# Moving the softmax inverse and two norms to other slots of a hand-ordered transformer block

## The chip, the cores and the metric

The kernel runs on one core of a Trainium2 chip. The core has a matmul engine (TensorE, PE in the profile), three engines for element-wise work (VectorE = DVE, ScalarE = ACT, GpSimd = POOL), and a queue engine (SyncE = SP) that here only issues transfers. ACT and POOL issue transfers too, each in its own instruction order. The metric is device microseconds (us) for one execution. Before the change the median of three runs is 2609.76 us (2608.44 to 2613.68).

## The reference

The input x is 4 sequences of 1024 tokens with 512 features, in float32. The kernel computes one transformer block conditioned on a vector, and adds its input once more at the end:

```
h  = g1(t) * x / sqrt(mean(x*x) + eps) + b1(t)
x1 = x + softmax(q k^T / sqrt(32)) v @ Wo.T      # 16 heads of 32, q, k, v from h
f  = g2(t) * x1 / sqrt(mean(x1*x1) + eps) + b2(t)
y  = x1 + (silu(f @ gate.T) * (f @ hid.T)) @ out.T   # hidden size 2048
return x + y
```

The two divisions of interest are the softmax's (by the sum over the 1024 keys, for each query and head) and the norms' (by a root mean square, for each token).

## The kernel before, in words

Tokens are cut into 8 blocks of 512 (two for each sequence). Everything is held with features on the 128 partitions. Attention goes by **groups** j = 0 to 63: a group is one block, 4 heads (128 feature rows) and 256 queries, so a block has 8 groups. A group has 4 **slots** (UN = 4), one for each 256 keys; the loop `while g < END` runs over slots g = 0 to 267. In the text, the *kind* of a slot is g % 4, and `p` followed by a number is its place in a block of 32 slots (p5 is g = 5 modulo 32; a block's attention starts at g = 32 n). The engines PE, DVE, ACT and POOL run in exactly the order in which the loop's body emits their instructions. SP's order is chosen by a scheduler, by the time at which it thinks each transfer can start.

A slot r passes through the engines as a software pipeline:

- In slot r, `scores` (line 284) multiplies keys by queries on PE, and `keep` (line 291) copies the result from PSUM to one of nine `raw` tiles on ACT. `running_max` (lines 296, 299) follows on DVE.
- In kind 0 of the next group, `max_T` (line 305) transposes the maxima on PE into the same PSUM tile that the scores use, and `parts` (lines 311 to 316) reduces them on DVE. In kind 1, `parts_T` (321) and `spread` (331, copied by ACT at line 332) bring them back as a `shift` to be added.
- Five slots after its scores, `shifted` (337, DVE) adds the shift and `exponential` (340, ACT) takes the exponential. Six slots after, `weighted` (350, PE) multiplies by the values, and `accumulate` (364) lets a transfer issued by POOL add this 1 MB tile into the group's first tile. Three such transfers belong to a group, each waiting for the landing of the one before.
- Three groups later (index j_n in the loop), `sums` (382, PE) sums over keys, after `fold_sum` (372, DVE) has added the halves at the end of the kind 3 before.

The inverse of the sums goes through memory, so that a reciprocal works on 128x8 numbers and not on 128x256: `sums_out` (387) copies and stores 4 KB (line 146, issued by ACT), `take` (152, ACT) loads them compactly, `invert` (157, DVE) takes the reciprocal, `put` (162, ACT) stores, `sums_in` spreads by four transfers of 32 KB (168, SP), and `normalize` (407, DVE) multiplies. Before the change the steps of group j sit in kinds 0, 1, 2, 3 of one group's slots and kinds 0 and 2 of the next: one slot for each transfer. The last two groups take the reciprocal directly on DVE (`inverse`, line 397).

Around the attention two other streams fill PE. Until slot 60 (FS), the projections of keys, queries and values are popped from a queue by `chain`; each batch half is first normalized (first norm: `norm_squares`, `norm_root`, reciprocal at line 613, `norm_scale` at 179, `norm_mod` at 182). From slot 60 on, the feed-forward network runs on the block before, one step for 128 hidden features every two slots (`pair_15` to `pair_4`, which multiply gate and hidden matrices by blocks with sums of blocks, and `contract`; `gate`, `hidden`, `sub_5`, `add_15` are theirs on DVE). Each block also has `project_out` (four chains from slot `go`), its residual, a second norm that goes through memory like the sums (`norm_compact`, `take`, `invert`, `put`, `norm_spread`), and `token_sums` (470 to 476). `pin`, `between` and `after` place a step at the head, middle or end of a slot. After slot 267 only the feed-forward network of the last block is left.

Every matmul of these is recorded at line 106 when it goes through the helper `mm`.

## Time and profile before

| what | value |
|---|---|
| median of 3 runs | 2609.76 us |
| the profiled execution | 2620.56 us, of it 2618.8 us from first to last instruction |
| mean granted clock of PE | 0.976 |
| busy: PE, DVE, ACT, POOL | 2435.8, 1846.6, 1406.9, 172.4 us |
| transfers | 510.64 MB, 195 GB/s |
| steady blocks (slots 96 to 127, for one) | 276.6 us |

PE is busy 93% of the span, so about 183 us of PE idle time and the time at a lowered clock are all that a new order of the same work can take away. The view of waits says which engine waited for whom; the view of windows gives busy time, the granted clock (PEclk) and the transfers' share for any stretch. A slot's length is read from the timeline as the time from the first score matmul (line 284) to the next slot's first.

### The profile page before, as it was taken

Reading aid. Unit: us, or ns where it says so; the run is one execution under the profiler, and the core shown is the slowest. Engines: PE = TensorE matmul, PEld = TensorE weight load, DVE = VectorE, ACT = ScalarE, POOL = GpSimd, SP = SyncE. Lnnn points to the kernel's source line nnn. Section 1 sums busy time; section 2 is a strip of 40 time slices with the busy share of each in tenths; the row PEclk is TensorE's granted clock in tenths of the full one; section 3 lists DMA queues with packets and bytes.
Section 4 is the critical chain, followed back from the end, with each engine's and each line's share of the span. In section 5 each row is a group of like instructions: output and inputs, shape, how many; then the busy total and the mean of one; then the engine's idle time right before and its main releaser. Section 6 shows DMA issues by size and latency. Waiting matters only on the chain. (4 is left out here: it accounts for less than half of the span.)

```text
span 2618.8 us, 71682 instructions
## 1 busy us (share of the span) xinstructions
PE 2435.8 (93%) x31785; PEld 1162.2 (44%) x31785; DVE 1846.6 (71%) x2180; ACT 1406.9 (54%) x1485; POOL 172.4 (7%) x207
## 2 busy tenths in 40 slices
PE   8989999898999999989998999899998999889999
PEld 3333333334544444444444454444444444444444
DVE  2677777766878877887878787887777777843322
ACT  3656676655556655555565565555565556522110
POOL 0000000000000000000000000000000000000000
PEclk9999999999999999999999999999999999999999
DMA  5698898977888888878877888788887888763442
GB/s 193 179 258 231 228 253 236 223 202 188 193 186 205 198 216 197 189 196 221 204 187 191 216 205 190 187 214 209 191 195 189 214 193 198 180 179 103 139 132 90
DMA packets 216386, 510.64 MB, mean 195 GB/s; under 512 B 43407, under 2 KB 84359, under 8 KB 188686
## 3 DMA queue, kind: packets, MB, share of 16 engines
q0 software_dynamic: 28656, 208.68, 41.1%
q1 hardware_dynamic: 166752, 296.56, 35.0%
q8 instruction: 250, 4.10, 0.6%
q10 hardware_dynamic: 20670, 0.83, 0.5%
q14 instruction: 58, 0.48, 0.1%
HBM read 254.82 MB, written 42.48 MB: 114 GB/s over the span
## 5 line engine op out<-in xcount | busy, mean ns | idle before, releaser
L337 DVE TENSOR_TENSOR raw<-raw,shift 128x2048 f32<-128x2048 f32 (+1 forms) x320 | 592.9, 1853 | 158.0 <-ACT shift L332 153.9
L291 ACT COPY raw<-sc 128x2048 f32<-128x2048 f32 x256 | 479.9, 1874 | 200.1 <-PE sc L284 88.4
L340 ACT ACTIVATE raw<-raw 128x2048 f32<-128x2048 f32 x256 | 490.9, 1918 | 110.0 <-DVE raw L337 109.2
L296 DVE TENSOR_TENSOR rmax<-rmax,raw 128x1024 f32<-128x1024 f32 x384 | 469.4, 1222 | 86.6 <-ACT raw L291 81.7
L106 PE MATMUL pc<-h,ow 128*32 128x512 f32 x4096 | 468.8, 595 | 0.0
L106 PE MATMUL pa<-x,fw 128*32 128x256 f32 x6144 | 394.1, 387 | 30.2 <-ACT shift L332 30.0
L284 PE MATMUL sc<-kq 32*128 32x256 f32 x4096 | 298.3, 406 | 2.8 <-ACT raw L291 2.8
L364 POOL DMA_DIRECT2D raw<-raw x192 | 165.3, 861 | 2040.3 <-ACT raw L340 991.7
L350 PE MATMUL av<-raw,v 128*32 128x256 f32 x4096 | 283.2, 394 | 9.2 <-ACT raw L340 9.2
L106 PEld LDWEIGHTS pa<-x,fw 128*32 128x32 f32 x6144 | 201.2, 111 | 182.7 <-ACT shift L332 40.5
L106 PE MATMUL pa<-sums,fw 128*32 128x256 f32 x4096 | 276.7, 388 | 0.0
L284 PEld LDWEIGHTS sc<-kq 32*128 32x128 f32 x4096 | 187.3, 186 | 143.7 <-issue 87.4
L106 PE MATMUL pkq<-y,wkq 128*32 128x512 f32 (+1 forms) x1664 | 238.3, 607 | 10.2 <-DMA wkq<-in_kq_w 6.0
L106 PEld LDWEIGHTS pc<-h,ow 128*32 128x32 f32 x4096 | 129.0, 110 | 243.2 <-issue 218.7
L106 PEld LDWEIGHTS pa<-sums,fw 128*32 128x32 f32 x4096 | 141.2, 113 | 88.3 <-issue 8.8
L350 PEld LDWEIGHTS av<-raw,v 128*32 128x32 f32 x4096 | 120.8, 111 | 121.8 <-issue 39.2
L538 ACT ACTIVATE t<-pa 128x512 f32<-128x512 f32 x128 | 78.0, 609 | 139.8 <-PE pa L106 136.9
L332 ACT COPY shift<-sp 128x512 f32<-128x512 f32 x128 | 75.0, 586 | 145.1 <-PE sp L331 96.6
L521 ACT COPY pb<-pa 128x256 f32<-128x256 f32 x128 | 45.8, 358 | 194.8 <-PE pa L106 178.8
L106 PE MATMUL pb<-sums,fw 128*32 128x256 f32 x2048 | 137.7, 387 | 12.9 <-DVE pb L528 12.9
L311 DVE TENSOR_REDUCE top<-mt 128x8 f32<-128x1024 f32 x64 | 78.3, 1223 | 96.8 <-PE mt L305 96.8
L559 DVE SCALAR_TENSOR_TENSOR res<-pc,res 128x512 f32<-128x512 f32 x128 | 88.3, 690 | 73.3 <-PE pc L106 73.3
(100 smaller groups left out, 1987.9 us busy)
## 6 DMA issues: line engine op xcount, KB each, us to landing
raw<-raw POOLq DMA_DIRECT2D x192, 1024.0 KB, 9.0
fw<-sw SPq DMA_DIRECT2D x256, 256.0 KB
ow<-in_out_w SPq DMA_DIRECT2D x128, 256.0 KB
fw<-in_gh_w SPq DMA_DIRECT2D x128, 256.0 KB
wkq<-in_kq_w SPq DMA_DIRECT2D x32, 512.0 KB
v<-vs SPq DMA_DIRECT2D x32, 512.0 KB
fw<-in_gh_w SPq DMA_DIRECT2D x128, 128.0 KB
kq<-kqs SPq DMA_DIRECT2D x31, 512.0 KB
```

What stands on the lines that cost most here:

```text
L106: nc.tensor.matmul(dst[k : k + n, :], w[:, k : k + n], moving, start=start, stop=stop, skip_group_check=seeded)
L284: nc.tensor.matmul(sc[:, i, k, :], t[rows, kt * P : (kt + 1) * P], t[rows, q0 : q0 + HQ], start=True, stop=True)
L291: nc.scalar.copy(raw[r].rearrange("p k h q -> p h k q"), state.pop(("sc", r)))
L296: nc.vector.tensor_tensor(rmax[j], rmax[j], raw[r][:, k, :, :], ALU.max)
L311: nc.vector.tensor_reduce(top, state.pop(("mt", j)), AX.X, ALU.max)
L332: nc.scalar.copy(shift[j][:, k : k + 2, :], pp)
L337: nc.vector.tensor_tensor(t, t, s.unsqueeze(1).to_broadcast(list(t.shape)), ALU.add)
L340: nc.scalar.activation(raw[r], raw[r], AF.Exp)
L350: nc.tensor.matmul(av[j][i * DH : (i + 1) * DH, :], v[m][:, kt, i * DH : (i + 1) * DH], raw[r][:, k, i, :], start=(kt == 0), stop=(kt == K ...
L364: nc.gpsimd.dma_start(out=acc[j].rearrange("p k h q -> p (k h q)"), in_=raw[r].rearrange("p k h q -> p (k h q)"), accum_op=ALU.add,)
L538: nc.scalar.activation(state["t", p], bank_a[p], AF.Tanh, scale=0.5)
L559: nc.vector.scalar_tensor_tensor(r, pp, 0.5, r, ALU.mult, ALU.add)
```

## The change

Seven things are done.

1. **Sums behind values.** In kind 0, `sums` is issued after `weighted` and `accumulate`, not ahead of them.
2. **Two slots for each transfer.** The inverse of a group's sums now takes: kind 0 `sums_out`; kind 2 `take`; end of kind 3 `invert`; next group's kind 0 `put`; end of its kind 1 `sums_in`; head of its kind 3 `normalize`.
3. **The last group of each block** (j % 8 == 7, and the last two) does not go through memory: DVE takes the reciprocal of the copied 128x256 tile in kind 1, and `normalize` follows in kind 2. `oT` is allocated by whichever of two groups comes first.
4. **Output projection** starts one slot earlier (`go` from g0 + 14 to g0 + 13), and in kind 1 its first chain comes after `pair_3`.
5. **Second norm** starts two slots earlier and is spread out: squares at p15 and p16, root at p17, load at p19, reciprocal at p20, store at p21, spread at p22, scaling by halves at p24 and p25; the first of the token sums at p25.
6. **First norm.** Its steps are aligned so that scaling falls into kind 2 (before: kind 0 for five of six), and it no longer follows the chain's start exactly; the two extra slots ahead of the last twelve chains are gone.
7. **Before slot 60**, the transposed maxima (`max_T`, `parts`) come ahead of the chain's eviction and the norm's steps.

```diff
+    def near(j: int):
+
+        return j % (C * NB // HQ) == C * NB // HQ - 1 or j >= NR // UN - 2
+
     def sums_out(j: int):
         t = sb.tile([P, HQ], F32, tag="rec", name=f"total{j}", bufs=2)
         nc.scalar.copy(t, state.pop(("sum", j)))
-        compact(f"s{j}", t, DH, HQ)
+        if near(j):
+            state["rec", j] = t
+        else:
+            compact(f"s{j}", t, DH, HQ)
...
-        if qh == 0:
+        if (n, hg) not in oT:
...
             s = math.ceil((len(queue) + 1) / PACE)
-            if s > BS + 15:
-                s += 2
+            s4 = s - 4 - (s - 6) % UN
             tag = f"a{b}_{half}"
-            pin(max(s - 10, 0), load_y, b, half)
+            pin(max(s4 - 6, 0), load_y, b, half)
             for k in range(2):
-                after(s - 8 + k, lambda b=b, half=half, tag=tag, k=k: norm_squares(y[b, half], tag, k))
-            between(s - 6, norm_root, tag)
-            after(s - 5, lambda tag=tag: nc.vector.reciprocal(state[tag], state[tag]))
+                after(s4 - 4 + k, lambda b=b, half=half, tag=tag, k=k: norm_squares(y[b, half], tag, k))
+            between(s4 - 2, norm_root, tag)
+            after(s4 - 1, lambda tag=tag: nc.vector.reciprocal(state[tag], state[tag]))
             for c in range(C):
-                between(s - 4, lambda b=b, half=half, tag=tag, c=c: norm_scale(y[b, half], tag, c))
-                after(s - 4 + c // 2, lambda b=b, half=half, c=c: norm_mod(0, b, y[b, half], c))
+                between(s4, lambda b=b, half=half, tag=tag, c=c: norm_scale(y[b, half], tag, c))
+                after(s4 + c // 2, lambda b=b, half=half, c=c: norm_mod(0, b, y[b, half], c))
...
-        go = g0 + (14 if n < NBLK - 1 else 8)
+        go = g0 + (13 if n < NBLK - 1 else 8)
...
-            after(g0 + 18, add_res, n)
+            after(g0 + 16, add_res, n)
             for k in range(2):
-                after(g0 + 17, lambda n=n, tag=tag, k=k: norm_squares(x2[n], tag, k))
-            between(g0 + 19, norm_root, tag)
-            between(g0 + 19, norm_compact, tag)
-            after(g0 + 20, take, tag)
-            between(g0 + 22, invert, tag)
-            after(g0 + 22, put, tag)
-            between(g0 + 24, norm_spread, tag)
+                after(g0 + 15 + k, lambda n=n, tag=tag, k=k: norm_squares(x2[n], tag, k))
+            between(g0 + 17, norm_root, tag)
+            between(g0 + 17, norm_compact, tag)
+            after(g0 + 19, take, tag)
+            between(g0 + 20, invert, tag)
+            after(g0 + 21, put, tag)
+            after(g0 + 22, norm_spread, tag)
             for c in range(C):
-                after(g0 + 25, lambda n=n, tag=tag, c=c: norm_scale(x2[n], tag, c))
-            for c in range(C):
-                between(g0 + 26, lambda n=n, c=c: norm_mod(1, n // QB, x2[n], c))
-            for i in range(3):
+                after(g0 + 24 + c // 2, lambda n=n, tag=tag, c=c: norm_scale(x2[n], tag, c))
+                after(g0 + 24 + c // 2, lambda n=n, c=c: norm_mod(1, n // QB, x2[n], c))
+            after(g0 + 25, token_sums, n, 0)
+            for i in range(1, 3):
                 after(g0 + 26, token_sums, n, i)
...
-            if kind == 0 and n_on:
-                sums(j_n)
-                if j_n >= direct:
-                    inverse(j_n)
+            if kind == 3 and o_on and not near(j_o):
+                normalize(j_o)
+            if kind == 2 and n_on and near(j_n) and j_n < direct:
+                normalize(j_n)
             if x_on and kind != 1:
                 shifted(r_x)
...
-            if kind == 0 and n_on and j_n >= direct:
-                normalize(j_n)
-            if kind == 2 and o_on:
-                normalize(j_o)
-            if kind == 1 and n_on and j_n < direct:
-                take(f"s{j_n}")
             for fn, a in pinned.pop(g, []):
                 fn(*a)
             if v_on:
                 weighted(r_v)
                 accumulate(r_v)
+            if kind == 0 and n_on:
+                sums(j_n)
+                if j_n >= direct:
+                    inverse(j_n)
+                    normalize(j_n)
...
-            if kind == 3 and n_on and j_n < direct:
-                put(f"s{j_n}")
-            if kind == 0 and o_on:
-                sums_in(j_o)
+            if kind == 1 and n_on and near(j_n) and j_n < direct:
+                nc.vector.reciprocal(state["rec", j_n], state["rec", j_n])
+            if kind == 2 and n_on and not near(j_n):
+                take(f"s{j_n}")
+            if kind == 0 and o_on and not near(j_o):
+                put(f"s{j_o}")
...
+                if kind == 0 and m_on:
+                    columns[0] = P
+                    max_T(j_m)
+                    parts(j_m)
                 if evict is not None:
                     evict()
                 for fn, a in halfway.pop(g, []):
                     fn(*a)
-                if kind == 0 and m_on:
-                    columns[0] = P
-                    max_T(j_m)
-                    parts(j_m)
...
-                if due or len(queue) > FG:
-                    chain(g)()
+                extra = due or len(queue) > FG
                 if kind == 3:
+                    if extra:
+                        chain(g)()
                     pair_7(p)
                     sub_5(p)
                 pair_3(p)
+                if kind == 1 and extra:
+                    chain(g)()
...
-            if kind == 2 and n_on and j_n < direct:
+            if kind == 3 and n_on and not near(j_n):
                 invert(f"s{j_n}")
+            if kind == 1 and o_on and not near(j_o):
+                sums_in(j_o)
```

## The prediction

> **What bounds the kernel now.** First the page, for what is busy:
>
> ```profile
> PE 2435.8 (93%) x31785; PEld 1162.2 (44%) x31785; DVE 1846.6 (71%) x2180; ACT 1406.9 (54%) x1485; POOL 172.4 (7%) x207
> ```
>
> PE bounds it. What can be won is its idle time (183 us) and time at a lowered clock: a mean of 0.976 over 2618.8 us is 63 us lost. Second the view of waits, cut to PE: who keeps it waiting?
>
> ```profile
> PE sum L382 <- issue: 36.0, 17, 7.5
> PE pa L106 <- ACT shift L332: 30.0, 11, 3.9
> PE sum L382 <- PE sc L284: 21.7, 23, 1.0
> PE pt L321 <- DVE split L316: 14.1, 6, 3.1
> PE pb L106 <- DVE pb L528: 12.9, 6, 2.2
> PE sum L382 <- DVE raw L372: 9.6, 9, 4.2
> ```
>
> The three `sum` rows make 67.3 us; then eleven stalls behind the shift copy. Third the timeline around one of each. A kind 1 (slot at 937.0):
>
> ```profile
> 942.76 0.32 ACTq L152 DMA_DIRECT2D fews<-sumss  x1
> ...
> 943.13 0.58 ACT L332 COPY shift<-sp 128x512 f32<-128x512 f32 x1 [4.19 <-DMA rec<-invss]
> ...
> 943.76 1.93 PE L106 MATMUL pa<-x,fw 128*32 128x256 f32 x16 [3.13 <-ACT shift L332]
> ```
>
> ACT stands at the issue of `take` (L152) and the copy queued behind it is late; PE waits 3.13 us, and then 16 matmuls take 1.93 us, where 16 of this size take 1.07 in the next fence. The releaser named is not the load's own input but the spread of another group. A kind 0:
>
> ```profile
> 1201.89 1.15 PE L284 MATMUL sc<-kq 32*128 32x256 f32 x16
> ...
> 1202.74 1.22 DVE L372 TENSOR_TENSOR raw<-raw 128x1024 f32<-128x1024 f32 x1
> ...
> 1204.06 0.64 PE L382 MATMUL sum<-raw,ones_sum 128*32 128x256 f32 x8 [1.02 <-PE sc L284]
> ...
> 1204.49 1.07 PE L350 MATMUL av<-raw,v 128*32 128x256 f32 x16
> ...
> 1205.26 1.87 ACT L291 COPY raw<-sc 128x2048 f32<-128x2048 f32 x1 [3.17 <-DMA raw<-raw]
> ```
>
> PE waits for DVE's fold while the values' matmuls, ready, stand behind. And `keep` waits until a 1 MB accumulation has landed. Fourth the windows (us, busy PE, PEld, DVE, ACT, POOL, clock, DMA share, GB/s): a steady block and the stalled kind 1.
>
> ```profile
> 894.50:1171.10 276.60, 259.70 (x3648) 130.46 (x3644) 218.57 (x257) 160.95 (x164) 21.48 (x25) 0.98 0.83 201
> ...
> 937.00:947.70 10.70, 7.57 (x101) 3.65 (x100) 4.99 (x5) 5.52 (x8) 0.86 (x1) 0.84 0.92 236
> ```
>
> DMA is at 0.83 and DVE at 218.57 of 276.6: both near enough to be next. Slot lengths from the timeline, undisturbed: kinds 0 to 3 take 9.91, 6.19, 7.24, 6.39 us.
>
> **The change, part by part.** Sums are against the profiled execution's 2620.56 us (10.8 above the median of 2609.76).
>
> *Two slots for each transfer.* Eleven kind-1 slots (p5, p25) last 46.6 us more than 11 x 6.19: 30.0 idle, the rest at a lowered clock. `take` goes to kind 2, a slot later; the spread goes to the end of kind 1, `put` to kind 0. The stores L146 landed in a median of 6.3 us, `put` in 7.8, each spread in 6.4 (latest 12.5; my reading of the semaphores' updates in the trace); a pair of slots is 13.6 us or more, so these waits go. What is late next: after p5 the accumulation chain. At p4 one took 12.4 us (1205.7 to 1218.1), the next 10.2; p8's `keep` needs the following one, which would share the DMA engines with them once PE comes 4.8 us earlier. I return 2 us for each of five blocks: 46.6 - 10 = 36.6.
>
> The Trainium skill ("DMA: Bandwidth & Descriptors", Anatomy of one DMA) puts a fixed cost of some 2.0 us on a transfer, which speaks against the change: a 4 KB store would be back within one slot, and two slots would win nothing here, so this term would be zero and the forecast 37 us later. [...]
>
> The lowered clock is in rows: PEclk 0.84 over the slot with a 3.13 us wait, and 0.76 over 1137.20 to 1151.30 after a wait of 2.12. The skill ("TensorE: Matmul & The Clock Gate", What's actually happening) lets the clock halve only after an idle window of about 3.4 us; by that most of these stalls would cost their idle time alone, 30.0 and not 46.6, and the term would be 20.
>
> *Sums behind values.* Values take 1.07 us and the fold ends about 0.9 us behind the scores, so up to 1.07 of each wait goes. But the transposed maxima of the same slot need `keep`'s PSUM tile. At 1207.2 they started 0.09 after `keep`'s end: PE would wait there instead. Taken slot by slot, the smaller of the wait and this slack sums to 27.6 us (4.1 before slot 64, 23.6 after; p0 and p4 give nothing, p28 1.07 each). Bounds 0 and 67.3; I take 24, as p8's 3 us fall under the return above.
>
> *Last group by VectorE.* Seven reciprocals of 128x256. Rows: 1758 ns (L397, from PSUM) and half of 3346 (L613, 128x512): 1.67 to 1.76 each, 12.3 in all, less 7 x 0.19. 49 transfers go. It stands in kind 1 behind the shift, with 2.2 us of DVE idle in an undisturbed kind 1 but 0.19 in kind 2, so kind 2's shift and exponential are late by over 1 us; the values in kind 3 have 0.94 of slack. Cost 0 to 12; I take 0.8 each: -5.6.
>
> *Second norm.* Six slots p27 are 19.7 us over 6.39, six p28 18.6 over 9.91 (7.5 of it in sums). There DVE does 2.74 us of scaling at once and three token sums, on top of the stall at p25. A group needs 27.5 us of DVE in 29.7; with scaling and token sums 33. Spread over p24 to p27 that still leaves about 3.5 us late per block: 30.8 - 21 = 10. Bounds 0 and 31. Its root moves from p19 to p17 with its 0.86 us of PE, its add (POOL) two slots up; SP's 256 KB spread moves from p24 to p22, ahead of p24's loads: cost nothing while SP waits for buffers anyway.
>
> *Output projection.* At p17 PE waits 1.57 us for the bank that the shift copy empties; behind `pair_3` the copy is done. 6 x 1.57 = 9.4; bounds 0 and 9.4, I take 8.
>
> *First norm.* Five pairs of slots with scaling in kind 0 last 26.8 us over 10.85 + 6.17, and slots 48 to 53, the one case with scaling in kind 2, 11.8 over undisturbed ones. One with kind 0, where DVE is busy 13.56 of 14.00 us and PE waits for it:
>
> ```profile
> 396.10:410.10 14.00, 10.78 (x95) 4.83 (x91) 13.56 (x18) 7.24 (x8) 1.72 (x2) 1.00 0.96 276
> ```
>
> Now 3.35 us of reciprocal and 2.74 of scaling fall into kinds 1 to 3, where DVE idles about 3 us; kind 0 idles 4.0. Some 3.3 us per norm stay: 38.6 - 20 = 18. Bounds: 38.6 if nothing is late, -32 if all six cost as slots 48 to 53 did (70.8). Loading y two to four slots earlier costs nothing where its buffer is empty; at slot 8 SP may stand a slot for it, with weights queued behind that PE's chains need two slots later. The maxima ahead of the norm's steps are what frees kind 0; behind them only evictions wait. The two dropped slots change nothing: the queue empties at 1.5 chains a slot behind the first projection, and the last twelve chains come out from slot 54 either way.
>
> *New waits.* `normalize` at the head of kind 3 holds back shift and exponential if the spread, issued one slot earlier, lands late; ACT's `take` now holds back `keep`. Rows: DVE waited 2.2 us once for a spread. Bounds 0 and what rival C prices; I take -8.
>
> Sum: 36.6 + 24 - 5.6 + 10 + 8 + 18 - 8 = 83. 2620.6 - 83 = 2537.6 profiled; less 10.8, **2527**.
>
> **Rivals.** *A, DMA sets the pace.* 0.83 share in a steady block would be 0.88 at 262 us; `keep` waited 81.0 us for accumulations already. Half of the first two terms, 10 for second norm and projection together, 5 for the first norm, and 15 for new waits: 23 + 12 - 6 + 10 + 5 - 15 = 29, so 2581. For it: p0 and p4 have no slack today. Against: p12 and p24 have 0.8 to 1.9.
>
> *B, everything fits.* No return at p5, sums 27.6, second norm 25, po 9, first norm 33, no new waits: 139, so 2471. Against it DVE's 27.5 of 29.7.
>
> *C, slower: the wait moves along with `take`.* The stalled ACT was released by a spread's landing, not by its own input. The spread now ends kind 1 and `take` opens kind 2; if ACT must again see a spread landed, it stands there with `keep` behind it and PE's next scores behind that, in up to 55 groups and not in eleven. Without the first term and the 8, the rest wins 54, so 1.0 us per group decides; at half of today's 4.6 it is 55 x 2.3 = 127 - 54: 2683. Against: the spread needed only 6.4 us, and today most `take`s issue without a stall.
>
> *D, no difference*, if gains and new waits cancel.
>
> **How the numbers follow.** Mine 0.60 (2495 to 2560), A 0.17, B 0.09, C 0.11, D 0.03. The range 2480 to 2600 leaves out C and most of B. A measurement tells 0.2% (5 us) from no change: faster 0.86, same 0.03, slower 0.11.
>
> **What would show it.** Waits of PE for `shift` (30.0) near zero; `sum` rows under 20 us, with some 15 more at `mt`; `pt` gone; steady blocks near 264 us; the clock's mean at 0.985 or more. Wrong if ACT waits at L152, or DVE at L407, in most groups, if `keep`'s wait for accumulations doubles, or if the values wait for the exponential in kinds 3 and 0.

## The result: no difference, and the profile after

The changed kernel takes 2616.32 us (median of 20 runs, 2604.63 to 2635.56), the kernel before 2616.57 (20 runs, 2608.44 to 2623.24) on the same chip. The ratio is 1.0002, with a 95% interval of 0.9984 to 1.002. A gain of 83 us was forecast and none came: the forecast of 2527 us is wrong, and the time lies outside its range of 2480 to 2600; rivals A (2581) and C (2683) miss it too, and only D, with 0.03, has the right time.

The profiled execution of the changed kernel took 2608.14 us, of it 2606.3 us of span, at a mean granted clock of 0.981 (before: 2620.56, 2618.8, 0.976). These two executions lie 12 us apart where the medians are equal; stretches of them are compared below with this in mind.

The page of the changed kernel, engines:

```profile
PE 2433.4 (93%) x31749; PEld 1143.4 (44%) x31749; DVE 1855.9 (71%) x2180; ACT 1405.5 (54%) x1483; POOL 172.9 (7%) x207
```

PE is idle for 173 us of the span, after 183. The stalls named by the prediction did go, so others came. The view of waits cut to PE, changed kernel (us in total, times, longest):

```profile
PE mt L305 <- ACT raw L291: 42.8, 28, 3.5
PE sum L382 <- issue: 24.7, 18, 6.4
PE av L350 <- ACT raw L340: 17.3, 21, 1.5
PE pmf L106 <- DVE h L550: 15.1, 6, 2.5
PE sp L331 <- ACT mT L323: 11.8, 8, 1.7
PE sc L284 <- ACT raw L291: 9.5, 6, 2.7
...
PE sum L382 <- DVE raw L372: 3.0, 3, 1.7
```

The 30.0 us at the shift copy and the 14.1 at `pt` are gone, and the rows of `sum` fell from 67.3 us to 27.7. In their place PE waits 42.8 us at the transposed maxima (`mt`) and 9.5 at the scores for the same thing, `keep`. In the kernel before these two rows were:

```profile
PE mt L305 <- ACT raw L291: 5.2, 7, 2.6
...
PE sc L284 <- ACT raw L291: 2.8, 3, 1.5
```

What `keep` itself waits for is in the page's list of groups; this is its row (busy, mean ns, then idle time ahead of it and what ended most of that) in the kernel before, and then in the changed one:

```profile
L291 ACT COPY raw<-sc 128x2048 f32<-128x2048 f32 x256 | 479.9, 1874 | 200.1 <-PE sc L284 88.4
```

```profile
L291 ACT COPY raw<-sc 128x2048 f32<-128x2048 f32 x256 | 479.3, 1872 | 277.3 <-DMA raw<-raw 153.7
```

Of `keep`'s idle time before, the largest share (88.4 of 200.1 us) was ended by PE's scores; 81.0 us ended with a transfer, as the prediction quotes. Now transfers end 153.7 us of it: the landing of 1 MB accumulations. By the times of these landings, 138.4 us (46 waits) are those of kind 0 and 15.4 us (8 waits) those of kind 1; before, all 81.0 us (35 waits) were those of kind 0. In each of them the accumulation is that of the slot seven back.

Windows of the changed kernel (us, busy PE, PEld, DVE, ACT, POOL, clock, DMA share, GB/s): the same steady block as before (slots 96 to 127), and slots p24 and p25 of the next block.

```profile
871.10:1149.30 278.20, 260.05 (x3648) 127.90 (x3644) 219.48 (x257) 160.69 (x164) 21.55 (x25) 0.98 0.82 198
1357.00:1371.70 14.70, 11.87 (x138) 5.50 (x134) 8.71 (x14) 4.58 (x5) 0.86 (x1) 0.88 0.95 253
1371.70:1381.30 9.60, 7.88 (x101) 3.65 (x100) 5.70 (x7) 6.46 (x8) 0.86 (x1) 0.82 0.68 145
```

The block takes 278.2 us where 264 were forecast and 276.6 were measured before. Slot p24, 11.07 us long in the kernel before, is 14.6 here, with the DMA engines at 0.95 and the clock at 0.88. Its timeline, with the slot ahead of it:

```profile
1351.09 0.86 POOL L364 DMA_DIRECT2D raw<-raw  x1 [9.94 <-ACT raw L340]
...
1352.72 0.32 SPq L263 DMA_DIRECT2D kq<-kqs  x1
...
1353.38 0.84 SPq L264 DMA_DIRECT2D kq<-kqs  x1
...
1357.05 1.15 PE L284 MATMUL sc<-kq 32*128 32x256 f32 x16
...
1359.15 0.64 PE L382 MATMUL sum<-raw,ones_sum 128*32 128x256 f32 x8
...
1362.43 1.87 ACT L291 COPY raw<-sc 128x2048 f32<-128x2048 f32 x1 [5.17 <-DMA raw<-raw]
...
1364.35 1.59 PE L305 MATMUL mt<-ident,rmax 128*128 128x128 f32 x8 [2.83 <-ACT raw L291]
```

In kind 3 POOL issues a 1 MB accumulation (1351.09). Slot p24 starts at 1357.05, values and sums are issued without a wait, and then `keep` stands for 5.17 us until that accumulation has landed (1362.33, by the semaphore's updates), because it writes into the tile that the accumulation reads. The maxima behind it need `keep`'s PSUM tile: PE idles 2.83 us. The accumulation took 11.2 us in the company of the keys' and queries' loads (768 KB, L263 and L264) and the second norm's spread, all issued within 4 us.

Where the time went is seen in slots. The table gives the mean length of stretches of a block, over the five blocks from slot 64 to 223 (from the starts of the score matmuls in the timeline), and the start of slot 64; the lower rows belong to the experiments. "Four parts" are parts 1, 2, 6 and 7 of the change.

| kernel | p0-3 | p4-8 | p9-12 | p13-19 | p20-23 | p24-28 | block | slot 64 |
|---|---|---|---|---|---|---|---|---|
| before | 32.2 | 47.9 | 30.8 | 66.2 | 30.3 | 51.0 | 278.2 | 608.5 |
| changed | 31.7 | 47.1 | 31.2 | 69.8 | 30.2 | 49.8 | 279.7 | 584.6 |
| sums alone | 32.1 | 46.2 | 30.1 | 66.2 | 30.1 | 49.2 | 273.6 | 596.6 |
| two slots alone | 33.0 | 45.3 | 30.8 | 66.2 | 31.3 | 47.9 | 274.3 | 603.4 |
| first norm alone | 32.0 | 47.8 | 30.8 | 66.2 | 30.3 | 51.1 | 278.0 | 588.6 |
| four parts | 32.0 | 46.8 | 30.3 | 66.2 | 31.1 | 47.3 | 273.5 | 589.8 |
| + last group | 32.2 | 47.1 | 31.2 | 66.1 | 31.2 | 47.3 | 274.9 | 590.2 |
| + projection | 32.0 | 47.5 | 31.5 | 68.6 | 30.0 | 47.6 | 277.0 | 595.1 |
| four parts, parted tiles | 30.9 | 44.2 | 30.4 | 66.5 | 31.7 | 46.2 | 269.7 | 584.4 |
| changed, parted tiles | 31.1 | 43.3 | 31.4 | 70.5 | 30.1 | 45.6 | 271.8 | 584.5 |
| best | 30.9 | 41.3 | 30.6 | 66.5 | 32.0 | 44.3 | 265.5 | 584.1 |
| four parts, half transfers | 29.9 | 41.2 | 29.9 | 66.2 | 29.7 | 45.6 | 262.4 | 564.0 |

(p29 to p31 take 19.8 or 19.9 in all of them.) Where the text gives the mean of a single slot, it is over six blocks, slots 64 to 255. The changed kernel is 24 us ahead at slot 64 and loses 1.5 us in each of these blocks; its profiled execution is one of its faster ones. The best kernel and the one with parted tiles and the spread norm alone have the same code up to slot 64 and start it at 584.1 and 589.8, so the last column is good to some 6 us.

### The profile page after: what moved, and what is told of

Same layout as the page of the kernel before. It is cut to its first block, busy times and chain, and to the rows that moved or that the text cites. A ratio compares the mean times of both kernels' runs of the same rounds, so it can differ in the third digit from the quotient of the medians.

```text
span 2606.3 us, 71466 instructions
## 1 busy us (share of the span) xinstructions
PE 2433.4 (93%) x31749; PEld 1143.4 (44%) x31749; DVE 1855.9 (71%) x2180; ACT 1405.5 (54%) x1483; POOL 172.9 (7%) x207
## 3 DMA queue, kind: packets, MB, share of 16 engines
q0 software_dynamic: 28656, 208.68, 41.4%
## 5 line engine op out<-in xcount | busy, mean ns | idle before, releaser
L291 ACT COPY raw<-sc 128x2048 f32<-128x2048 f32 x256 | 479.3, 1872 | 277.3 <-DMA raw<-raw 153.7
L106 PE MATMUL pc<-h,ow 128*32 128x512 f32 x4096 | 476.9, 603 | 2.3 <-DVE rec L404 2.1
L106 PE MATMUL pa<-sums,fw 128*32 128x256 f32 x4096 | 269.5, 380 | 0.0
L350 PEld LDWEIGHTS av<-raw,v 128*32 128x32 f32 x4096 | 108.0, 110 | 143.1 <-issue 49.9
L106 PEld LDWEIGHTS pkq<-y,wkq 128*32 128x32 f32 (+1 forms) x1664 | 74.4, 119 | 147.4 <-issue 122.6
```

The lines of the kernel that those rows point to most:

```text
L106: nc.tensor.matmul(dst[k : k + n, :], w[:, k : k + n], moving, start=start, stop=stop, skip_group_check=seeded)
L291: nc.scalar.copy(raw[r].rearrange("p k h q -> p h k q"), state.pop(("sc", r)))
L350: nc.tensor.matmul(av[j][i * DH : (i + 1) * DH, :], v[m][:, kt, i * DH : (i + 1) * DH], raw[r][:, k, i, :], start=(kt == 0), stop=(kt == K ...
```

## The experiments

All medians are of several runs beside the kernel before on the same chip. Gains are given as (1 - ratio) x 2616 us, so that runs of different chips can be compared; the 95% intervals of the ratios are some 0.002 to either side, 4 to 7 us. The kernels with half transfers leave out half of each tile that is added, so their sums over keys are incomplete.

| kernel | us | ratio, 95% interval | gain, us |
|---|---|---|---|
| changed | 2616.32 | 1.0002 (0.9984 to 1.002) | 0 |
| sums alone | 2578.02 | 0.985 (0.9827 to 0.9872) | 39 |
| two slots alone | 2593.27 | 0.9915 (0.9888 to 0.9942) | 22 |
| first norm alone | 2599.24 | 0.9926 (0.9903 to 0.995) | 19 |
| four parts (1, 2, 6, 7) | 2574.89 | 0.9833 (0.9807 to 0.9858) | 44 |
| + last group by VectorE (3) | 2584.80 | 0.9873 (0.9848 to 0.9897) | 33 |
| + projection (4) | 2592.43 | 0.9903 (0.988 to 0.9925) | 25 |
| changed, kind 0's order altered | 2613.58 | 0.9987 (0.9965 to 1.001) | 3 |
| changed, `norm_mod` later | 2598.64 | 0.9941 (0.9923 to 0.9958) | 15 |
| before, half transfers | 2543.36 | 0.9728 (0.9704 to 0.9752) | 71 |
| four parts, half transfers | 2479.96 | 0.9489 (0.9466 to 0.9511) | 134 |
| changed, half transfers | 2512.31 | 0.9594 (0.957 to 0.9618) | 106 |
| four parts, load pinned to p10 | 2571.97 | 0.984 (0.9816 to 0.9864) | 42 |
| before, parted tiles | 2610.55 | 0.9987 (0.997 to 1.0004) | 3 |
| four parts, parted tiles | 2545.95 | 0.9742 (0.9719 to 0.9765) | 67 |
| changed, parted tiles | 2558.02 | 0.9793 (0.9774 to 0.9811) | 54 |
| four parts, parted, load moved | 2536.58 | 0.9702 (0.9687 to 0.9717) | 78 |
| four parts, parted, norm spread | 2534.79 | 0.97 (0.9683 to 0.9716) | 78 |
| best: all three | 2523.12 | 0.9657 (0.9636 to 0.9678) | 90 |

### The parts one at a time

The theory after the first look at the traces was that of an exchange of tiles. The nine `raw` tiles come back in the order in which they are freed. Before, kind 1's `keep` took the tile that the sums had just freed, and had no transfer to wait for; in the changed kernel it takes the tile of the slot seven back, whose accumulation was issued only one slot earlier.

The first edit was meant to bring the old order back:

```diff
             if v_on:
                 weighted(r_v)
-                accumulate(r_v)
             if kind == 0 and n_on:
                 sums(j_n)
...
+            if v_on:
+                accumulate(r_v)
```

> The changed kernel with one order altered: in kind 0 the sums come behind the values but ahead of `accumulate`, as the freed tiles then come back in the order of before: kind 1's `keep` gets the group's first tile and not the one whose 1 MB transfer was issued a slot earlier. Theory T (tiles): the lost gain sits in this exchange. The wait of `keep` for transfers falls from 153.7 us to 100 or less, PE's waits for `keep` ahead of scores (9.5) and for the exponential ahead of values (17.3) mostly go, and the time is 15 to 30 us under the changed kernel's 2616, so 2586 to 2601. Theory P (pace): the transfers of a group are late as a chain, whichever tile is asked for first; the time stays within 0.3% of 2616 and PE's wait at the transposed maxima (42.8) stays or grows.

Measured: 2613.58 us, ratio 0.9987, no difference that counts. But the edit did not do what it was for: in its trace kind 1's `keep` still waits for the accumulation of the slot seven back (at slot 133, 3.18 us until 1209.00, issued 1195.4). So it says nothing for or against the exchange; it only shows that the order of the sums and `accumulate` costs nothing that can be measured.

The other three take one part each into the kernel before. Sums alone:

```diff
-            if kind == 0 and n_on:
-                sums(j_n)
...
                 weighted(r_v)
                 accumulate(r_v)
+            if kind == 0 and n_on:
+                sums(j_n)
```

> The kernel before with part 1 alone: sums behind values and behind `accumulate`. The prediction's term says 24 us faster than before, 2592. Theory T: the exchange of tiles comes with this part, so `keep`'s wait for transfers goes from 81.0 to some 130 us or more and the 67 us of PE's waits at the sums come back at the transposed maxima and at the next scores: 2608 to 2625. Theory P says 2605 to 2616, with the wait moved to the maxima of the same slot but `keep`'s row little changed.

Two slots for each transfer alone (the projection's chains stay at p15 and p17):

```diff
-            if kind == 2 and o_on:
-                normalize(j_o)
-            if kind == 1 and n_on and j_n < direct:
-                take(f"s{j_n}")
...
+            if kind == 3 and o_on:
+                normalize(j_o)
...
+            if kind == 2 and n_on and j_n < direct:
+                take(f"s{j_n}")
+            if kind == 0 and o_on:
+                put(f"s{j_o}")
```

> The kernel before with part 2 alone: two slots for each transfer of the sums' inverse, all groups through memory; the output projection's first chain moves from slot 14 to 15 since the last group is normalized a slot later. The prediction's terms say 36.6 less 8 for new waits, so about 28 us faster: 2588. Theory T: nothing is exchanged here, so the gain is there: 2580 to 2595, with the 30.0 us at the shift copy gone. Theory P: the time stands at 2605 to 2616, since p5 runs into the chain of transfers at p8 and the gain is lost by then.

First norm alone (parts 6 and 7, as in the change's diff):

> The kernel before with parts 6 and 7 alone: the first norm aligned, and the transposed maxima ahead of evictions before slot 60. The prediction's term is 18 us; in the changed kernel's trace slot 64 starts 24 us earlier, of which the sums' part has some 4. So 2592 to 2600 if what is won there stays won: nothing behind slot 64 differs. If it is lost again behind slot 64 (a later start of transfers or of the clock), 2610 to 2616.

Measured: gains of 39, 22 and 19 us. Theory T fell with the first of them: sums alone carry the exchange of tiles too (one `keep` of kind 1 waits there for the accumulation of the slot seven back, 0.7 us; none did before), and win more than the prediction gave them. PE's waits with sums alone:

```profile
PE sum L382 <- issue: 15.0, 7, 6.4
...
PE mt L305 <- ACT raw L291: 11.1, 14, 1.6
...
PE sum L382 <- DVE raw L372: 0.8, 1, 0.8
```

The three `sum` rows went from 67.3 us to 15.8, and only 5.9 of it came back at `mt` (5.2 to 11.1). Each part does, alone, about what was forecast for it or better (24, 28.6 and 18 us); the sum of the three gains is 81 us, uncertain by some 11.

### The parts together

Four kernels lead from the three parts to the whole change: four parts; with the last group by VectorE (`near` as in the change); with the projection one slot earlier; and, as the last, the changed kernel itself, which adds the second norm. Beside them stands the changed kernel with halved accumulations:

```diff
-                out=acc[j].rearrange("p k h q -> p (k h q)"),
-                in_=raw[r].rearrange("p k h q -> p (k h q)"),
+                out=acc[j][:, 0, :, :].rearrange("p h q -> p (h q)"),
+                in_=raw[r][:, 0, :, :].rearrange("p h q -> p (h q)"),
```

> The kernel before with parts 1, 2, 6 and 7, all groups through memory; the output projection stays in slots 15 and 17 and the second norm where it was. Alone these parts won 40.8 (sums), 25.5 (two slots) and 19.5 us (first norm). Theory A (adding): the gains add, 86 us, so 2525 to 2545, and parts 3 to 5 cost some 80 us. Theory C (collision): two freed stalls run into the same chain of transfers, so 2555 to 2580 and parts 3 to 5 cost the other half. Theory N: nothing is left once parts 1 and 2 meet, 2600 or more, and parts 3 to 5 cost little.

> The same with part 3 as well: the last group of a block inverted by VectorE, the output projection's weights asked for at slot 11 as before. The prediction's cost for part 3 is 5.6 us; the changed kernel's slot 10 is 0.8 us longer in each of six blocks, 4.9 in all. Theory A and N: 3 to 8 us over the kernel without part 3. Theory C, if the 49 fewer transfers make room: 0 to 10 us under it.

> The same with part 4 as well, so the changed kernel with only the second norm in its old places. By the prediction part 4 wins 8 us. If parts 3 to 5 cost what the result lacks and the second norm is the costly one (its squares, root, spread and scaling move PE's waits to slot 17 and the transfers to slot 24), this one is 30 us or more under the changed kernel's 2616. If the output projection in slot 13 is the costly one (the changed kernel's slots 13 to 19 take 44.5 us and not 41.8, 16 us in six blocks), this one is within 10 us of 2616.

> The changed kernel with each 1 MB `accumulate` cut to its first half, 0.5 MB: the second halves of three of four tiles are left out of the sums over keys, so this part of the computation is missing. Everything is issued in the same order. If late accumulations are what the changed kernel waits for, `keep`'s wait for transfers falls from 153.7 us to under 40, and the time falls by the 42.8 us at the maxima, most of the 9.5 and 17.3, and some clock: 2540 to 2565. If the order of PE's and VectorE's own work is what costs, 2590 to 2616.

Measured: the four parts together win 44 us, not 81: Theory C, a collision, though at its edge. Parts 3, 4 and 5 then cost 10, 8 and 26 us one after the other (differences of the gains, each uncertain by some 8), and the change is at zero. The second norm is the costliest, but not alone.

The collision is seen in the table. In the five steady blocks sums alone, two slots alone and both together take 273.6, 274.3 and 273.5 us: the second of the two edits wins nothing there. Ahead of slot 64 the gains are 11.9, 5.1 and 19.9 alone and 18.7 together. Together the waits look like this, in the timeline of slots p4 to p6 of one block (four parts):

```profile
1173.91 1.87 ACT L291 COPY raw<-sc 128x2048 f32<-128x2048 f32 x1 [3.39 <-DMA raw<-raw]
1174.04 0.33 SPq L418 DMA_DIRECT2D res<-in_x  x1
1174.33 0.86 POOL L364 DMA_DIRECT2D raw<-raw  x1 [9.11 <-issue]
...
1187.69 1.86 ACT L291 COPY raw<-sc 128x2048 f32<-128x2048 f32 x1 [2.90 <-DMA raw<-raw]
...
1188.20 0.86 POOL L364 DMA_DIRECT2D raw<-raw  x1 [13.01 <-DMA raw<-raw]
...
1189.61 1.15 PE L284 MATMUL sc<-kq 32*128 32x256 f32 x16 [1.85 <-ACT raw L291]
```

At p4 `keep` is late by a first accumulation (3.39). The next is issued at 1174.33, in one breath with the 1 MB load of the residual (L418), and lands at 1187.67, after 13.3 us. Kind 1's `keep` needs its tile and stands 2.90 us; PE's next scores, behind it, 1.85. The kernel before had the same company at p4 (load at 1205.39, accumulation at 1205.68, 12.4 us), and PE did not wait for it there: the stall that `take` caused in p5 was time in which these transfers caught up. Without it, PE meets them one slot later.

With half transfers the changed kernel falls by 106 us to 2512.31, more than was expected of it. The row of accumulations in the page's list of DMA issues (KB each, median us to landing), whole and halved, and `keep`'s row, halved:

```profile
raw<-raw POOLq DMA_DIRECT2D x192, 1024.0 KB, 9.0
```

```profile
L291 ACT COPY raw<-sc 128x2048 f32<-128x2048 f32 x256 | 479.4, 1873 | 162.3 <-PE sc L284 124.4
...
raw<-raw POOLq DMA_DIRECT2D x192, 512.0 KB, 5.6
```

`keep` now mostly waits for PE's scores, 124.4 of its 162.3 us, and for accumulations 5.6 us, after 153.7. They are what the changed kernel waits for. But halving them helps any version, so two more kernels were halved, and the suspected load was pinned to another slot:

> The kernel before with each `accumulate` cut to its first half, as was done to the changed kernel (2616 to 2512): the second halves of three of four tiles are missing from the sums over keys. If the transfers of the accumulations are what swallows the change's gain, the change is worth its 83 us once they are short: 2512 + 83 = 2595, so 2580 to 2605 here. If the change had no gain to swallow, this kernel falls by the same 104 us as the changed one: 2505 to 2525.

> The kernel with parts 1, 2, 6 and 7 (2575) with each `accumulate` cut to its first half: the second halves of three of four tiles are missing from the sums. It tells whether parts 3 to 5 cost by themselves or through late transfers. By themselves: 2512 less the 41 us between 2575 and 2616, about 2471. Through transfers alone: 2505 to 2515. From the changed kernel's rows, what stays without transfers is slot 10 (0.8), the projection and root in slots 13 to 19 (2.7) and the wait at slot 25 (2.7), less what slots 27 and 28 win (3 to 4): 1 to 3 us in each of six blocks, so I expect 2495 to 2510.

Measured: before 2543.36, four parts 2479.96, changed 2512.31. With short transfers the change wins 35 us (gains 71 and 106), the four parts 63, and parts 3 to 5 cost 28 by their own order. That is more than the 1 to 3 us a block I gave them: the blocks differ by 4.6 us (262.4 and 267.0), of it 4.3 in p13 to p19. It is not the 83 either, in part because short transfers already free `take`: in the halved kernel before p5 lasts 6.19 us, and nothing is left there to win.

```diff
-        pin(g0 + 6, load_res, n)
+        pin(g0 + (10 if n < NBLK - 1 else 6), load_res, n)
```

> The kernel with parts 1, 2, 6 and 7 (2575), with one transfer of each of the first seven blocks moved: the 1 MB load of the residual is pinned to slot 10 and not 6. In the trace that load was issued at slot 4 together with an accumulation that then took 13.3 us, where the others take 8 to 9. Theory: this company is what makes the maxima of slot 4, the scores of slot 6 and the maxima of slot 8 late (slots 4 to 8 take 46.7 us in the mean, and 40.6 with halved accumulations). Then slots 4 to 8 lose 3 to 5 us a block and the time is 2545 to 2560. If the accumulations are late there for another reason, or the load disturbs slots 10 to 12 as much, 2570 to 2580.

Measured: 2571.97 us, no gain, and the load did not move. SP still issued it at p4 (1170.76 in this trace), beside an accumulation of 13.4 us. SP's order is the scheduler's; the pin moved the call, not the transfer. What the load's company costs stayed open with this run.

### Parting the tiles

Kind 0's `keep` takes the tile of slot g - 7, whose accumulation POOL issued in the kind 3 just before (so at p24 above, and at slot 132 in the four-part kernel: issued 1164.4, landed 1173.8). This was so before the change too. The edit gives the first tiles of groups, which the sums set free, three buffers of their own, and the others six:

```diff
-        raw[r] = sb.tile([P, 2, HG, HQ], F32, tag="raw", name=f"raw{r}", bufs=RAW)
+        first_of = r % UN == 0
+        raw[r] = sb.tile(
+            [P, 2, HG, HQ], F32, tag="acc" if first_of else "raw", name=f"raw{r}", bufs=3 if first_of else RAW - 3
+        )
```

> The kernel with parts 1, 2, 6 and 7 (2575), with the nine tiles parted: three for the first tiles of groups, six for the others. Kind 0's `keep` then takes the tile that the sums of the same slot set free, and no longer the one whose accumulation was issued a slot earlier; kinds 1 to 3 take tiles whose accumulation was issued two slots earlier. Theory: PE's waits at the maxima (26.6), the scores (9.3) and part of those at the values (28.0), and the clock behind them, are this order of tiles; `keep`'s wait for transfers falls from 119 us to under 40 and the time to 2530 to 2555. Against it: `keep` of kind 0 then stands behind PE's sums, which end some 3 us into the slot, so the maxima may be as late as today in every group: 2575 to 2600.

> The changed kernel, all seven parts, with the tiles parted: three for the first tiles of groups, six for the others. The kernel with parts 1, 2, 6 and 7 fell by 29 us to 2546 by this edit. If parts 3 to 5 cost only through late accumulations, which this takes away, 2540 to 2555. If they cost by their own order too, as with halved accumulations (2512 against 2480, 32 us), 2570 to 2585. If the changed kernel's loss is all in that order, 2605 or more. Slot 24, 14.0 us in the changed kernel, should be under 11, and slot 25 stay at 8.9 or more.

> The kernel before with only the tiles parted: three for the first tiles of groups, six for the others. By my present theory the order of tiles became the bound when the other stalls went: before, `keep` waited 81 us for transfers, but PE only 5.2 us at the maxima and 2.8 at the scores, so 2600 to 2616 here, and the stalls at `take` and the sums stay. Rival: it held the kernel before as much as the changed one, hidden in the waits named `sum`: 2560 to 2590.

Measured: four parts 2545.95 (a gain of 67 and no longer 44), changed 2558.02 (54 and no longer 0), before 2610.55 (3, within its interval of no change). So the order of tiles did not hold the kernel before, it took 23 us of the four parts' gain and 54 of the changed kernel's. What parts 3 to 5 cost beside it is 13 us, between the two cases that were expected. In the trace of the changed kernel with parted tiles, slot p24 reads:

```profile
1333.24 0.86 POOL L367 DMA_DIRECT2D raw<-raw  x1 [9.99 <-ACT raw L343]
...
1334.05 0.32 SPq L263 DMA_DIRECT2D kq<-kqs  x1
...
1338.32 1.15 PE L284 MATMUL sc<-kq 32*128 32x256 f32 x16
...
1340.72 0.38 PE L385 MATMUL sum<-raw,ones_sum 128*32 128x256 f32 x1
...
1341.14 1.87 ACT L294 COPY raw<-sc 128x2048 f32<-128x2048 f32 x1 [2.62 <-PE sum L385]
...
1343.06 1.09 PE L308 MATMUL mt<-ident,rmax 128*128 128x128 f32 x8 [0.23 <-ACT raw L294]
```

The accumulation issued at 1333.24 landed only at 1346.1, later than in the fence of the changed kernel (12.9 us), and nobody waits for it here: `keep` starts with the end of the sums (2.62 us of idle time on ACT, for PE), and PE waits 0.23 us at the maxima. Cut to PE, the waits are (lines moved by three, so L308 is `mt` and L294 is `keep`):

```profile
PE sum L385 <- issue: 28.6, 23, 6.4
PE pmf L106 <- DVE h L553: 15.1, 6, 2.5
...
PE av L353 <- ACT raw L343: 12.6, 14, 1.5
PE mt L308 <- ACT raw L294: 11.8, 46, 0.3
...
PE sc L284 <- ACT raw L294: 1.0, 1, 1.0
```

`mt` falls from 42.8 to 11.8, and the scores from 9.5 to 1.0. The price is 0.23 to 0.3 us in nearly every group at the maxima (46 times). The edit also takes kind 1 from the tile of seven slots back to that of eight; by the waits above (138.4 and 15.4 us) nearly all of it should be kind 0's, but no run parted the two.

### The residual's load and the second norm

Issued by ACT, whose order is the program's, the load does move (in blocks 1 to 6):

```diff
+        if 0 < n < NBLK - 1:
+            after(g0 + 9, load_res, n)
+        else:
+            pin(g0 + 6, load_res, n)
...
+        queue = nc.scalar if 0 < n < NBLK - 1 else nc.sync
+        queue.dma_start(out=res[n], in_=x[n])
```

> Parts 1, 2, 6 and 7 with parted tiles (2546), and the 1 MB load of the residual issued by ACT at the end of slot 9 in blocks 1 to 6, so that it does move. Theory: its company makes slots 4 and 7 to 8 late (11.86, 7.18 and 11.55 us, against 10 to 10.6, 6.39 and 10.1 with halved accumulations). Then 3 to 4 us a block go: 2524 to 2532. If the load makes slots 10 to 12 late instead, 2540 to 2550.

Measured: 2536.58 us; 11 us more than with parted tiles alone (gains 78 and 67, the intervals of the ratios do not meet). Slots p4 to p8 fall from 44.2 to 41.4 us, the 41.2 of half transfers, and the accumulation at p4 takes 9.4 us in the block shown above (slot 132) and not 13.2. p9 to p12 rise by 0.5. The gain is a little less than expected. The load was not moved in the kernel before, so how much of these 11 us that one would win too is not known.

Two runs look at the second norm. In the changed kernel, its last ACT step issued later:

```diff
-                after(g0 + 24 + c // 2, lambda n=n, c=c: norm_mod(1, n // QB, x2[n], c))
+            for c in range(C):
+                between(g0 + 25 + c // 2, lambda n=n, c=c: norm_mod(1, n // QB, x2[n], c))
```

> The changed kernel with the second norm's last ACT step (`norm_mod`) issued half a slot to a slot later, in the middle of slots 25 and 26 and not at the end of 24 and 25. In the changed kernel's trace PE waits 1.72 us in slot 25 for the copy of the shift's parts, which stands behind these on ACT, with a lowered clock behind it. Theory: this order is a part of the second norm's cost; slot 25 falls from 9.7 to 7 us or less and slots 26 to 28 give back up to 1 us: 10 to 18 us in six blocks, 2598 to 2606. Rival: slot 24's wait for the accumulation lowers the clock anyhow and only 1.7 us a block go: 2604 to 2610; or the token sums come later and PE waits for them in slots 27 and 28: 2612 to 2620.

In the four-part kernel with parted tiles, the later half of part 5 with its root left at p19:

```diff
-            between(g0 + 22, invert, tag)
-            after(g0 + 22, put, tag)
-            between(g0 + 24, norm_spread, tag)
+            between(g0 + 21, invert, tag)
+            after(g0 + 21, put, tag)
+            after(g0 + 22, norm_spread, tag)
...
-                after(g0 + 25, lambda n=n, tag=tag, c=c: norm_scale(x2[n], tag, c))
+                after(g0 + 24 + c // 2, lambda n=n, tag=tag, c=c: norm_scale(x2[n], tag, c))
...
-                between(g0 + 26, lambda n=n, c=c: norm_mod(1, n // QB, x2[n], c))
+                between(g0 + 25 + c // 2, lambda n=n, c=c: norm_mod(1, n // QB, x2[n], c))
```

> Parts 1, 2, 6 and 7 with parted tiles (2546), and of part 5 only its second half: squares, root and load where they were before (slots 17 to 20), reciprocal and store in slot 21, spread at the end of 22, scaling by halves at the end of 24 and 25, `norm_mod` in the middle of 25 and 26, the first token sum at 25. If spreading VectorE's work is worth what the prediction gave it (10 us and more) and only the root's place and the late accumulation spoiled it, slots 27 and 28 (22.4 us) fall to 19 and the time is 2525 to 2538. If the spread's company or VectorE's order in slots 24 to 26 costs what they win, 2543 to 2555.

Measured: 2598.64 us, a gain of 15, and 2534.79, 11 more than without the spreading. In the first, p25 falls from 9.7 to 6.19 and p27 gives 1.3 back; p24 stays at 14.0 to 14.3, as its wait is the accumulation's. In the second, p24 to p28 fall from 46.2 to 44.5 us. Slots 27 and 28 take 20.3 us where 19 were expected. So spreading the scaling is worth what the prediction gave it, 10 us, once ACT's steps stand behind the shift copy of p25 and the root stays in a kind 3.

Last, all of it in one kernel: four parts, parted tiles, moved load, spread norm.

> Parts 1, 2, 6 and 7, parted tiles, the residual's load moved to slot 9 by ACT (alone 9 us, 2537), and the second norm's transfers and scaling spread as in k0_split_norm (alone 11 us, 2535). If they add, 2523 to 2530. If both relieve the same slots (27, 28 and what follows at 0 and 4), 2530 to 2537.

Measured: 2523.12 us, ratio 0.9657 (0.9636 to 0.9678), the fastest. Its steady block in the view of windows:

```profile
855.30:1118.20 262.90, 254.92 (x3644) 126.98 (x3640) 218.14 (x257) 160.47 (x164) 21.50 (x25) 1.00 0.85 211
```

262.9 us, at full clock, and with a DMA share of 0.85 where the kernel before had 0.83 over 276.6. In the steady blocks a share of 0.83 was not what set the pace; the place where the program waited for the transfers was. Ahead of slot 64 this is not shown: there the four parts with half transfers are another 20 us earlier (564.0 and 584.1). And p20 to p23 take 32.0 us in the fastest kernel, 30.2 in the changed one, for the second norm's `take` (below); its earlier place was not tried in the fastest kernel.

## Why the prediction was wrong, step by step

The 83 us that did not come are, in the order in which the parts were added: 27 for the three parts together (70.6 forecast, 44 measured), 4 for the last group, 16 for the projection and 36 for the second norm. Two steps of the prediction failed: it added up savings that hang on one chain of transfers, and it priced at nothing steps of the second norm that, at their new places, make PE wait.

**Two slots for each transfer** (36.6, less 8 for new waits): 22 alone (15 to 29). The effect is there: p5 and p25, 10.6 and 9.5 us, become 6.19, and `normalize` holds nobody back. The reason given for it, a transfer that needs more than one slot, is not what the eleven stalls show. ACT's waits in the kernel before have this row, which is gone with two slots alone:

```profile
ACT shift L332 <- DMA rec<-invss: 39.9, 10, 5.0
```

In all eleven, `take`'s own 4 KB store had landed 3.8 to 7.1 us before `take` was issued (by the semaphores); ACT stood until another group's spread had landed, 8.7 to 12.5 us after its issue, as the prediction had read off for one of them. So the gain came from parting `take` and that spread, not from the second slot; which of the moves did it was not told apart. The spread itself still has one slot, from the end of kind 1 to the head of kind 3. It is rival C's mechanism, and it comes back, but once a block and not in every group: with two slots alone and with four parts, the second norm's `take` at the end of p20 stands 4.8 us on ACT until another group's store, issued 7 us earlier in the same slot, has landed (1317.81 and 1324.47, by the semaphores). In the timeline of the kernel with four parts, the copy of the shift's parts stands behind it and PE behind that:

```profile
1317.81 0.50 ACTq L146 DMA_DIRECT2D sumss<-total  x1
...
1324.82 0.33 ACTq L152 DMA_DIRECT2D fewf<-sumsf  x1
1325.19 0.36 ACT L323 COPY mT<-pt 12x256 bf16<-12x256 bf16 x1 [1.97 <-issue]
1325.60 0.37 PE L331 MATMUL sp<-mT,select 12*128 12x256 bf16 x2 [1.21 <-ACT mT L323]
```

p20 to p23 take 31.1 to 31.3 us there and not 30.3. The changed kernel issues that `take` at p19 and is free of it (30.2). With the stalls goes more than their idle time (at p5 4.4 us for 2.7), so the lowered clock behind a wait of 3 us was real. Windows of the changed kernel, for the wait of 2.83 us at p24 and what follows:

```profile
1361.38:1364.79 3.41, 0.58 (x8) 0.45 (x5) 0.53 (x1) 2.14 (x2) 0.00 (x0) 1.00 0.98 363
1364.79:1368.20 3.41, 3.41 (x18) 1.34 (x20) 2.09 (x6) 2.18 (x2) 0.86 (x1) 0.50 0.84 195
```

The clock is at 0.50 for 3.41 us and then full again; half of 3.41 is 1.7 us, which is what p5 lost beyond its idle time. The Trainium skill ("TensorE: Matmul & The Clock Gate", What's actually happening) lets the clock halve only after an idle window of some 3.4 us. Here it halves behind a wait of 2.83 us, and in p25 (1375.03 to 1378.44) behind one of 1.72, so the rows disagree with the page. The skill ("DMA: Bandwidth & Descriptors", Anatomy of one DMA) gives a fixed cost of some 2.0 us for a transfer of the gpsimd path. The stores of the eleven stalls, issued by ACT, landed 4.0 to 7.6 us after their issue, so that figure is too low for them under this load. What was given back at p8 is there as forecast (10.9 to 12.8 us).

**Sums behind values** (24): 39 alone. The waits at the sums fell by 51.5 and those at the maxima rose by 5.9, where the slack counted from the rows of before let only 27.6 go. The slot-by-slot minimum took `keep`'s end as fixed; p4, given nothing, won 0.7 us and p28 1.7.

**First norm** (18): 19. Right in size and place: all of it lies ahead of slot 64.

**Their sum** is the step that failed first. The prediction had the collision in its hands ("after p5 the accumulation chain") and priced it at 10 us, 2 for each of five blocks at p8. It is 37, uncertain by some 12: some 20 in the steady blocks, the rest ahead of slot 64, where no run told its waits apart. Each stall's price had been worked out with all other stalls in place, and they were the time in which the accumulations landed. Parting the tiles gives 23 of the 37 back. Rival A had this mechanism and halved two terms for it; that is nearly what happened to the four parts (2575 measured, 2581 forecast for A), without the cost of parts 3 to 5. (Its 23 is half of 46.6; half of the term of the sum, 36.6, would be 18. B's terms, with the last group's -5.6, come to 136 and not 139.) Its reason was the wrong one: the DMA share did not bound the steady blocks, and the order of nine tiles took the larger part. The prediction took `keep`'s waits of before as given, and did not price which tile each kind would get; its own sign, `keep`'s wait for accumulations doubling, all but came true (81.0 to 153.7).

**Last group by VectorE** (-5.6): -10, with 8 of uncertainty. p10 is 0.82 us longer in each block, as priced.

**Output projection** (+8): -8. The wait of 1.57 us at p17 does go, and the first chain behind `pair_3` finds its bank free, as forecast. But the bank that it holds is the one that `pair_15` needs, 0.81 us late for the eviction (L433), and the second chain of p13 waits for the slot's gate. PE's waits with parts 1 to 4, 6 and 7:

```profile
PE po L106 <- DVE h L550: 6.0, 7, 0.9
PE pa L106 <- DVE x L433: 5.7, 7, 0.8
```

That is 0.85 us a block at p13 and 0.81 at `pa`, 1.66 for the 1.57 that went. Then p19, which had cost nothing, has PE idle for 2.10 us, 1.83 of it for the exponential ahead of the values. p13 to p19 take 68.6 us and not 66.2. In one block (slots 145 to 147) ACT runs the four squares of the second norm (0.6 us each) in p18 there, ahead of `keep` and that exponential; the changed kernel has them at p15 and p16, and its p19 takes 6.4 us and not 9.6. The prediction looked at the one bank that the chain takes, and not at who needs it next.

**Second norm** (+10): -26. Two steps priced at nothing cost the most. The root at p17:

```profile
1307.59 1.05 PE L106 MATMUL pb<-sums,fw 128*32 128x256 f32 x16
...
1310.31 0.69 DVE L550 SCALAR_TENSOR_TENSOR h<-t,pa 128x512 f32<-128x512 f32 x1
...
1311.14 1.07 PE L106 MATMUL pmf<-totf,ones_mean 128*32 128x512 f32 x8 [2.51 <-DVE h L550]
```

PE stands 2.51 us in each block. The root's PSUM bank is held until the slot's `gate` (L550), which in a kind 1 comes behind the exponential and the next products; in a kind 3, where the root was, `gate_tanh` comes earlier and the wait is 0.27. The spread, moved "ahead of p24's loads" at no cost, now travels with them and with the accumulation for which p24 waits. With only the second norm in its old places that accumulation took 8.1 us and p24 10.3; with part 5 it takes 11.2 and p24 14.0, of it 2.78 PE's wait. (That the company is the reason was not tested by moving the spread alone.) And `norm_mod` ahead of the shift's parts on ACT costs 15 us by the run that moved it. What was forecast as the gain is there: p27 falls from 9.7 to 7.3 us and p28 from 13.0 to 11.3.

The 27.5 us of DVE in a group, held against rival B, played no part: DVE is at 218 us in the fastest block, as it was before.

## What to carry to other kernels

Stalls on one path are not independent savings. Take away two and ask what ran on in the background during them, here a chain of three 1 MB transfers in each group, and price both removals against that chain together. For every copy that waits for "a buffer", write down which buffer the rotation hands it and who frees that one: nine tiles in one pool made the most urgent copy of a group wait for the youngest transfer, and parting them was worth 54 us to the changed kernel and 3, not clear of nothing, to the kernel before. A step that is moved takes its banks with it: look at who holds the PSUM bank at the new place, and at what stands behind it on the same engine.

## What was not expected of the hardware

- The same 1 MB accumulation lands in a median of 9.0 us, and in 11 to 13 us in the company of another 1 MB load, or of 768 KB of loads and a spread. Moving one 1 MB load by five slots brought 13.2 us down to 9.4 in one block and won 11 us, with the same bytes moved.
- Idle times well under 3.4 us halve the clock. From 600 to 2300 us of the changed kernel's trace the clock was halved 18 times, always behind 3.41 us in which PE had been busy for 17 to 50%; cut on into stretches of this length, the trace has two more as idle as that (46 and 50%) that were not followed by it. In the mean PE idles 4.5 us in p24 and p25 of the changed kernel, and the two are 7.6 us longer than undisturbed slots of their kinds (9.91 and 6.19). In the fastest kernel the clock is 1.00 over a block and 0.993 over the span.
- A transfer's place in the program said little about its time on SP: a load pinned four slots later was issued at the same place, 3.5 us into p4 (3.7 without the pin).
